# Cross attention: exponentials turned on VectorE in squares of 32 and moved between partitions by transfers, in place of transposes on TensorE

## The chip, the cores and the metric

One core of one Trainium2 chip. The metric is device time in microseconds (us) of the whole program, the median over several executions. Five engines work side by side: TensorE (PE in the profile, with PEld for its weight loads), VectorE (DVE), ScalarE (ACT), GpSimd (POOL) and SyncE (SP), whose queue issues all DMA transfers of this kernel. Each engine has its own queue of instructions and runs it in order; semaphores tie them together.

## The reference, cut to what matters

The program is a two-layer decoder in float32 on 8 batches of 128 tokens by 512 features: attention, an autocorrelation against a context and a mixture of low-rank experts in the first layer; attention, cross attention and a low-rank sum in the second, each with a residual and a layer norm. The change touches the cross attention of the second layer alone:

```python
B, Q, D = (8, 64, 512)
H, KV, HD = (16, 4, 96)
G = H // KV
b, q_len, _ = latents.shape                      # 8, 128
hidden = jnp.concatenate([context, latents], axis=1)   # 256 keys
q = (latents @ Wq.T).reshape(b, q_len, H, HD)
k = (hidden @ Wk.T).reshape(b, s_len, KV, HD)
v = (hidden @ Wv.T).reshape(b, s_len, KV, HD)
...
scores = jnp.einsum('bkgqd,bksd->bkgqs', q, k) * scale
attn = jax.nn.softmax(scores.astype(jnp.float32), axis=-1).astype(q.dtype)
out = jnp.einsum('bkgqs,bksd->bkgqd', attn, v)
out = out.reshape(b, H, q_len, HD).transpose(0, 2, 1, 3).reshape(b, q_len, H * HD)
return out @ Wo.T
```

Each of the 16 query heads has 128 queries against 256 keys; four query heads (G) share one of four key heads (KV).

## The kernel before

The kernel is written in a tile framework: tiles come from pools with a fixed number of buffers, and the framework derives all semaphores. It also orders each engine's instructions, by the order of the text and by when it reckons that operands are ready; so on ACT and DVE, and at places on PE, an instruction can stand before one that the text has earlier. The change leaves everything up to line 866 as it is.

**Cross attention.** Batches go in pairs (`pr`, `j`). A `Front` holds one pair's projections: transposed tokens xTx, context tokens cT (one DMA on SP, L749), values v, keys kT and queries qT. Its `pieces` (14 of them: tokens, four of values, three of keys, six of queries) are work that is cut up, so that `nxt.go(n)` puts n pieces of the next pair on PE between the steps of the present one.

**Heads8** is half a batch: two of the four query heads of each key head, so eight score maps (index j = 2g + u, with g the key head and u the head of the half). Its steps are:

- `__init__`: 48 matmuls s_x (L878) write the scores, 128 queries by 8 x 256 keys, into two PSUM tiles of two banks.
- `maxima` (L889, L890): two reductions of 1024 per lane on DVE.
- `exps(half)` for each of two halves: four exponentials on ACT (L900) with their row sums, a reciprocal on DVE (L904) and four multiplications in place (L906). The tile e is `[128, 8, 256]`: queries in partitions, then head, then key.
- `turn(pT)` brings the keys into partitions: for each g four transposes on PE (L915) into one PSUM bank, and an eviction of 128x512 into pT, by DVE for even g (L921) and by ACT for odd g (L923).

A batch has two Heads8 (hh = 0 and 1), the whole stage has 16. The tile pT has one buffer, e has two.

**mixed** (L932): with all of pT there, 48 matmuls o_x multiply the values with it, 32 output features of four key heads at a time, and three evictions write oT (L937). **projection** (pox, L86 within `mm_acc`) multiplies with the output weights, 24 matmuls, then `add_norm`. Together these two are `mix`, and a batch's `mix` runs in the next batch's first half, for the last batches later: the mix of batch 5 in batch 6's second half, that of batch 6 in batch 7's second half and that of batch 7 at the end.

**The loop** (L1015 to L1061) sets the order: in a batch's first half scores, the turn of the previous half (passed to `maxima`, which keeps the reductions behind it), exponentials, one piece, the previous batch's `mix`, one or two pieces; in its second half scores, first exponentials, three pieces, the turn of the first half, the other exponentials, two pieces. Batches 6 and 7 (`b >= B - 2`) have no next pair; there `low_rank()`, the small stage behind cross attention (xTf, pl, lT, pof), takes the place of the pieces.

**SP's queue** in this stage carries the cT load of each next pair (L749, when a `Front` is made) and the stores of finished batches (L992, L1082).

Of the kernel before, what the change touches and what calls it, by code (L numbers as in the profile page):

```python
# [17 lines left out]
P = 128  # L18
# [25 lines left out]
def decoder(ctx: ExitStack, tc: tile.TileContext, a: dict, out: bass.AP):  # L44
# [809 lines left out]
    with stage("x1b", 2, side="right") as ap, stage("f1", 2, side="right") as fp:  # L854
# [12 lines left out]
        class Heads8:  # L867

            def __init__(self, qT, kT, h0, name):
# [12 lines left out]
            def maxima(self, behind=None):  # L884

                self.m = sm.tile([P, 8], F32, tag="mx", name=f"m_{self.name}")
                with tc.issue_after(behind.ins) if behind else nullcontext():
                    for i in range(2):
                        nc.vector.tensor_reduce(self.m[:, 4 * i : 4 * i + 4], self.s[i], AX.X, ALU.max, negate=True)  # L889
                    nc.vector.tensor_scalar(self.m, self.m, 1.0 / math.sqrt(XD), None, ALU.mult)  # L890
                self.e = ap.tile([P, 8, 2 * P], F32, tag="e", name=f"e_{self.name}")
                self.su = sm.tile([P, 8], F32, tag="sux", name=f"su_{self.name}")
                self.rc = sm.tile([P, 8], F32, tag="rcx", name=f"rc_{self.name}")

            def exps(self, half):

                js = slice(4 * half, 4 * half + 4)
                for i in range(4):
                    j = 4 * half + i
                    nc.scalar.activation(  # L900
                        self.e[:, j, :], self.s[half][:, i, :], AF.Exp,
# [3 lines left out]
                for j in range(4 * half, 4 * half + 4):  # L905
                    nc.vector.tensor_scalar(self.e[:, j, :], self.e[:, j, :], self.rc[:, j : j + 1], None, ALU.mult)  # L906

            def turn(self, pT):

                for g in range(KV):  # L910
                    pt = bank(f"pt_{self.name}_{g}")
                    for s in range(2):
                        for u in range(2):
                            i = 2 * s + u
                            nc.tensor.transpose(  # L915
                                pt[:, i * P : (i + 1) * P], self.e[:, 2 * g + u, s * P : (s + 1) * P], ident
                            )
                    o = pT[:, :, g, self.h0 : self.h0 + 2, :].rearrange("p s u t -> p s (u t)")
                    i = pt.rearrange("p (s x) -> p s x", s=2)
                    if g % 2 == 0:  # L920
                        copied = nc.vector.tensor_copy(o, i)  # L921
                    else:
                        nc.scalar.copy(o, i)  # L923
                return copied

        def mixed(b, v, pT, oT):

            for n in range(NS):
                po = bank(f"o_x1_{b}_{n}")
                for s in range(2):  # L930
                    for g in range(KV):
# [3 lines left out]
                            rhs=pT[:, s, g].rearrange("p h t -> p (h t)"), start=(s == 0), stop=(s == 1),  # L935
                        )
                (nc.scalar.copy if n == 1 else nc.vector.tensor_copy)(oT[:, n, :], po)  # L937
# [57 lines left out]
        nxt = prev = None  # L995
# [19 lines left out]
        for b in range(B):  # L1015
# [4 lines left out]
            for hh in range(2):  # L1020
                now = Heads8(front.qT[:, :, toks], front.kT[:, :, :, toks], 2 * hh, f"x1_{b}_{hh}")
                if b >= B - 2:

                    now.maxima()
                    now.exps(0)
                    if hh == 0:
                        low_rank()
                        prev.turn(pT)
                        now.exps(1)
                        low_rank()  # L1030
                    else:
                        mix()
                        pT = ap.tile([P, 2, KV, G, P], F32, tag="pT", name=f"pT_x1_{b}", bufs=1)
                        prev.turn(pT)
                        now.exps(1)
                elif hh == 0:
                    now.maxima(prev.turn(pT) if prev else None)
                    now.exps(0)
                    now.exps(1)
                    if j == 0:  # L1040
                        nxt = Front(pr + 1)

                    nxt.go(1)
                    if mix:
                        mix()
                    nxt.go(1 + j)
                else:
                    now.maxima()
                    now.exps(0)
# [183 lines left out]
```

## Time and profile before

| | |
|---|---|
| median of 3 runs | 923.43 us (923.0 to 924.23) |
| the profiled execution | 920.14 us, of which its instructions span 918.3 us |
| granted TensorE clock, mean over the span | 0.996 |
| L915, transposes of e | 256, on PE 31.5 us busy together |
| L900, exponentials | 128 of 128x256, 488 ns each |
| L932, o_x | 384, 43.6 us busy together |
| L86, pox | 192, 84.5 us busy together |
| L749, cT load | 512 KB, lands 3.8 us after its issue |

Profile lines are read so: a line of kernel.py, the engine, the operation, the tile that it writes and those that it reads, shapes, how often; then busy time in us and the mean of one in ns; then the engine's idle time just before these instructions, and which engine and line ended it. In the chain of waits a piece is its start in us, its length in us, the engine, tile and line, and how many instructions. Times within the profile count from the first instruction of the profiled execution; its own time also holds what lies around the span.

Cross attention runs from 543 us to 901 us: s_x starts at 543.12, and the last pox ends at 901.2.

### The profile page before, as it was taken

To read this page: it belongs to the slowest core of one execution; us is meant where nothing else is said; L and a number is where in the kernel's file an instruction comes from. 1 tells how busy PE (TensorE), PEld (TensorE's weight loads), DVE (VectorE), ACT (ScalarE), POOL (GpSimd) and SP (SyncE) were. 2 spreads that over 40 slices of the span, in tenths; PEclk is the share of its full clock that TensorE was granted. 3 is DMA by queue.
4 is the path that set the end of the run, shared out by engine and by line. 5 is a ranking of instruction groups with operands and counts; after the bars stand their busy time and mean duration, and the time that the engine had idled before them with its cause. 6 is when DMAs were issued, how large, how long until landed. Compare 5 with 4: busy or idle time off the path is not lost.

```text
span 918.3 us, 17042 instructions
## 1 busy us (share of the span) xinstructions
PE 885.4 (96%) x6750; PEld 559.4 (61%) x6750; DVE 547.0 (60%) x1294; ACT 379.6 (41%) x1549; POOL 166.3 (18%) x235
## 2 busy tenths in 40 slices
PE   9999999899899999999999999999999999999985
PEld 5766656564445455565556787585758575865552
DVE  3757788886867668888887215433433353355544
ACT  3876564644232136666666022233223322334220
POOL 2401233233432423344330000000000000000001
PEclk9999999999999999999999999999999999999998
DMA  9700000121200020000030200000000000000000
GB/s 329 301 2 24 2 24 2 58 94 60 91 1 23 1 69 25 2 1 2 2 138 25 70 1 1 24 1 1 1 24 1 1 1 1 1 13 0 24 24 35
DMA packets 9298, 34.40 MB, mean 37 GB/s; under 512 B 1154, under 2 KB 1282, under 8 KB 7298
## 3 DMA queue, kind: packets, MB, share of 16 engines
q1 hardware_dynamic: 9218, 33.31, 10.0%
q8 instruction: 53, 0.87, 0.4%
q14 instruction: 27, 0.22, 0.1%
HBM read 31.21 MB, written 2.10 MB: 36 GB/s over the span
## 4 chain that ended last, share of the span: by engine, by line
PE 79%; DVE 10%; ACT 8%; issue 1%; POOL 1%; DMA 0%; POOLq 0%; SPq 0%; ACTq 0%; DVEq 0%
PE pox L86 9%; PE pqx L86 9%; PE pq L86 5%; PE s_x L878 5%; ACT e_a L193 5%; PE pk L86 5%; PE o_x L932 5%; PE pv L86 5%; PE pkx L86 5%; PE pvx L86 4%; PE pof L86 4%; PE pt_a L212 3%; PE pt_x L915 3%; PE s_a L164 2%; PE po L665 2%; PE o_a L229 1%
## 5 line engine op out<-in xcount | busy, mean ns | idle before, releaser
L193 ACT ACTIVATE e_a<-e_a,m_a 128x128 f32<-128x128 f32 (+1 forms) x512 | 184.8, 365 | 113.8 <-DVE m_a L181 113.8
L193 ACT ACTIVATION_READ_ACCUMULATOR e_a<-e_a,m_a 128x1 f32 x512 | 97.3, 190 | 0.0
L900 ACT ACTIVATE e_x<-s_x,m_x 128x256 f32<-128x256 f32 x128 | 59.1, 488 | 79.1 <-DVE m_x L890 79.1
L86 PE MATMUL pqx<-xTx,w_X_q 128*128 128x256 f32 x384 | 84.8, 380 | 0.0
L86 PE MATMUL pox<-w_X_o,oTx 128*128 128x512 f32 x192 | 84.5, 596 | 0.0
L86 PEld LDWEIGHTS pqx<-xTx,w_X_q 128*128 128x128 f32 x384 | 72.5, 190 | 11.9 <-issue 2.4
L889 DVE TENSOR_REDUCE m_x<-s_x 128x4 f32<-128x1024 f32 x32 | 37.6, 1217 | 54.1 <-PE s_x L878 54.1
L86 PEld LDWEIGHTS pox<-w_X_o,oTx 128*128 128x128 f32 x192 | 35.8, 190 | 48.8 <-issue 44.6
L97 POOL TENSOR_TENSOR rs_x<-ve_x,neghalf 128x1 f32<-128x1 f32 x8 | 4.4, 548 | 324.1 <-DVE ve_x L95 324.1
L181 DVE TENSOR_REDUCE m_a<-e_a 128x4 f32<-128x512 f32 (+1 forms) x128 | 62.6, 542 | 0.0
L792 ACT COPY qTx<-pqx 128x512 f32<-128x512 f32 x24 | 14.1, 588 | 105.8 <-PE pqx L86 105.8
L212 PE MATMUL pt_a<-ident,e_a 128*128 128x128 f32 x384 | 48.6, 274 | 4.9 <-DVE e_a L352 3.9
L878 PE MATMUL s_x<-kTx,qTx 32*128 32x256 f32 x768 | 50.3, 384 | 1.4 <-ACT e_x L900 1.4
L212 PEld LDWEIGHTS pt_a<-ident,e_a 128*128 128x128 f32 x384 | 43.5, 141 | 12.8 <-DVE e_a L352 4.9
L103 DVE TENSOR_TENSOR x_x<-pox,x_a 128x512 f32<-128x512 f32 x8 | 5.5, 692 | 70.5 <-PE pox L86 70.5
L923 ACT COPY pT_x<-pt_x 128x512 f32<-128x512 f32 x32 | 18.8, 591 | 67.8 <-PE pt_x L915 67.6
L878 PEld LDWEIGHTS s_x<-kTx,qTx 32*128 32x128 f32 x768 | 39.9, 184 | 11.2 <-issue 6.4
L932 PE MATMUL o_x<-pT_x,vx 128*32 128x512 f32 x384 | 43.6, 594 | 0.0
L921 DVE COPY pT_x<-pt_x 128x512 f32<-128x512 f32 x32 | 22.0, 687 | 32.0 <-PE pt_x L915 31.9
L164 PEld LDWEIGHTS s_a<-kbd,qT 32*64 32x64 f32 x1024 | 20.7, 131 | 28.1 <-issue 8.9
L906 DVE TENSOR_SCALAR e_x<-e_x,rc_x 128x256 f32<-128x256 f32 x128 | 36.5, 348 | 1.1
L164 PE MATMUL s_a<-kbd,qT 32*64 32x256 f32 (+1 forms) x1024 | 33.2, 335 | 1.8 <-DVE pT_a L213 0.8
(209 smaller groups left out, 1707.6 us busy)
## 6 DMA issues: line engine op xcount, KB each, us to landing
w_X_q<-in_X_q SPq DMA_DIRECT2D x3, 1024.0 KB, 5.1
w_X_o<-in_X_o SPq DMA_DIRECT2D x3, 1024.0 KB, 5.0
w_L_Wv<-in_L_Wv SPq DMA_DIRECT2D x2, 1024.0 KB, 6.3
w_L_Wo<-in_L_Wo SPq DMA_DIRECT2D x2, 1024.0 KB, 8.0
x_in<-in_x SPq DMA_DIRECT2D x8, 256.0 KB, 7.9
ct<-in_ctx SPq DMA_DIRECT2D x8, 256.0 KB, 4.4
cT<-in_ctxT SPq DMA_DIRECT2D x4, 512.0 KB, 3.8
out<-x_f SPq DMA_DIRECT2D x8, 256.0 KB, 2.0
```

Of the source, the lines that this page charges most:

```text
L86: nc.tensor.matmul(ps, lhsT=l, rhs=r, start=(i == 0), stop=(i == n - 1))
L164: nc.tensor.matmul(s[r // 2][64 * u : 64 * u + 64, r % 2, cols], lhsT=qT[rows, 64 - 64 * part : P - 64 * part], rhs=kbd[rows, :, :keys], s ...
L181: self.scored = nc.vector.tensor_reduce(self.m[:, part, rs, :], self.by_heads(part)[:, rs], AX.X, ALU.max, negate=True)
L193: nc.scalar.activation(e[:, r, x, :], e[:, r, x, :], AF.Exp, bias=self.m[:, part, r, x : x + 1], accum_out=self.su[:, part, r, x : x + 1],)
L212: nc.tensor.transpose(pt[:, r, cols], self.e[:, 2 * i + r, cols], ident)
L878: nc.tensor.matmul(sc[g // 2][:, g % 2, u * 256 : (u + 1) * 256], lhsT=qT[rows, (h0 + u) * NS + n, :], rhs=kT[rows, n], start=(n == 0), st ...
L889: nc.vector.tensor_reduce(self.m[:, 4 * i : 4 * i + 4], self.s[i], AX.X, ALU.max, negate=True)
L900: nc.scalar.activation(self.e[:, j, :], self.s[half][:, i, :], AF.Exp, bias=self.m[:, j : j + 1], scale=1.0 / math.sqrt(XD), accum_out=sel ...
L906: nc.vector.tensor_scalar(self.e[:, j, :], self.e[:, j, :], self.rc[:, j : j + 1], None, ALU.mult)
L915: nc.tensor.transpose(pt[:, i * P : (i + 1) * P], self.e[:, 2 * g + u, s * P : (s + 1) * P], ident)
L921: copied = nc.vector.tensor_copy(o, i)
L932: nc.tensor.matmul(po[32 * g : 32 * g + 32, :], lhsT=v[:, s, g * XD + 32 * n : g * XD + 32 * n + 32], rhs=pT[:, s, g].rearrange("p h t -> ...
```

## The change

The exponentials are laid out so that a key block of 32 is the outer index: e becomes `[128, 8, 8, 32]`, that is key block, head, key within the block. ACT and DVE write and read it in runs of 32 elements.

After the four multiplications of a half, one DVE transpose over `[128, 8, 4, 32]` turns every square of 32 queries by 32 keys in place: partition 32i + k then holds key 32a + k of block a, for the 32 queries of block i. What is left is to bring the square of key block a to the partitions 32 (a mod 4) and on. `turn` does that with 16 transfers on SP's queue, one for each pair (i, j) of query block and key block modulo 4: 32 partitions by two runs of 1 KB, 64 KB each, from e to pT. The tile pT becomes `[128, 2, 4, 2, 256]`: key half, query block, half of the heads, and head by query within the block.

`mixed` reads pT with runs of 64 columns, and its evictions put the columns back into the order that `projection` expects, in runs of 32.

The loop no longer carries a `prev`: a turn stands right after the second exponentials of its own half. In a batch's first half it stands behind the previous batch's `mix`, because pT has one buffer; in batches 6 and 7 both turns stand in the second half, behind `mix`. The reductions are no longer held behind a turn.

```diff
--- before.py
+++ after.py
@@ -868,6 +868,7 @@
 
 
 
+
             def __init__(self, qT, kT, h0, name):
                 self.h0, self.name = h0, name
                 sc = [banks(f"s_{name}_{i}") for i in range(2)]
@@ -881,14 +882,12 @@
                             )
                 self.s = [t.rearrange("p g (u k) -> p (g u) k", u=2) for t in sc]
 
-            def maxima(self, behind=None):
-
+            def maxima(self):
                 self.m = sm.tile([P, 8], F32, tag="mx", name=f"m_{self.name}")
-                with tc.issue_after(behind.ins) if behind else nullcontext():
-                    for i in range(2):
-                        nc.vector.tensor_reduce(self.m[:, 4 * i : 4 * i + 4], self.s[i], AX.X, ALU.max, negate=True)
-                    nc.vector.tensor_scalar(self.m, self.m, 1.0 / math.sqrt(XD), None, ALU.mult)
-                self.e = ap.tile([P, 8, 2 * P], F32, tag="e", name=f"e_{self.name}")
+                for i in range(2):
+                    nc.vector.tensor_reduce(self.m[:, 4 * i : 4 * i + 4], self.s[i], AX.X, ALU.max, negate=True)
+                nc.vector.tensor_scalar(self.m, self.m, 1.0 / math.sqrt(XD), None, ALU.mult)
+                self.e = ap.tile([P, 8, 8, 32], F32, tag="e", name=f"e_{self.name}")
                 self.su = sm.tile([P, 8], F32, tag="sux", name=f"su_{self.name}")
                 self.rc = sm.tile([P, 8], F32, tag="rcx", name=f"rc_{self.name}")
 
@@ -898,30 +897,22 @@
                 for i in range(4):
                     j = 4 * half + i
                     nc.scalar.activation(
-                        self.e[:, j, :], self.s[half][:, i, :], AF.Exp,
+                        self.e[:, :, j, :], self.s[half][:, i, :].rearrange("p (a k) -> p a k", k=32), AF.Exp,
                         bias=self.m[:, j : j + 1], scale=1.0 / math.sqrt(XD), accum_out=self.su[:, j : j + 1],
                     )
                 nc.vector.reciprocal(self.rc[:, js], self.su[:, js])
                 for j in range(4 * half, 4 * half + 4):
-                    nc.vector.tensor_scalar(self.e[:, j, :], self.e[:, j, :], self.rc[:, j : j + 1], None, ALU.mult)
+                    e = self.e[:, :, j, :]
+                    nc.vector.tensor_scalar(e, e, self.rc[:, j : j + 1], None, ALU.mult)
+                nc.vector.transpose(self.e[:, :, js, :], self.e[:, :, js, :])
 
             def turn(self, pT):
-
-                for g in range(KV):
-                    pt = bank(f"pt_{self.name}_{g}")
-                    for s in range(2):
-                        for u in range(2):
-                            i = 2 * s + u
-                            nc.tensor.transpose(
-                                pt[:, i * P : (i + 1) * P], self.e[:, 2 * g + u, s * P : (s + 1) * P], ident
-                            )
-                    o = pT[:, :, g, self.h0 : self.h0 + 2, :].rearrange("p s u t -> p s (u t)")
-                    i = pt.rearrange("p (s x) -> p s x", s=2)
-                    if g % 2 == 0:
-                        copied = nc.vector.tensor_copy(o, i)
-                    else:
-                        nc.scalar.copy(o, i)
-                return copied
+                e = self.e.rearrange("p (s j) h k -> p s j (h k)", s=2)
+                for i in range(4):
+                    for j in range(4):
+                        nc.sync.dma_start(
+                            pT[32 * j : 32 * j + 32, :, i, self.h0 // 2, :], e[32 * i : 32 * i + 32, :, j, :]
+                        )
 
         def mixed(b, v, pT, oT):
 
@@ -932,9 +923,13 @@
                         nc.tensor.matmul(
                             po[32 * g : 32 * g + 32, :],
                             lhsT=v[:, s, g * XD + 32 * n : g * XD + 32 * n + 32],
-                            rhs=pT[:, s, g].rearrange("p h t -> p (h t)"), start=(s == 0), stop=(s == 1),
+                            rhs=pT[:, s].rearrange("p i h x -> p (i h) x")[:, :, 64 * g : 64 * g + 64],
+                            start=(s == 0), stop=(s == 1),
                         )
-                (nc.scalar.copy if n == 1 else nc.vector.tensor_copy)(oT[:, n, :], po)
+                (nc.scalar.copy if n == 1 else nc.vector.tensor_copy)(
+                    oT[:, n, :].rearrange("p (h i t) -> p i h t", h=4, i=4),
+                    po.rearrange("p (i h t) -> p i h t", i=4, h=4),
+                )
 
         def projection(b, oT):
             po = bank(f"pox_{b}")
@@ -992,7 +987,7 @@
             nc.sync.dma_start(out[b], y)
 
         front.go(14)
-        nxt = prev = None
+        nxt = None
         done, tokens_low, scores_low = [], [], []
 
         def low_rank():
@@ -1019,40 +1014,36 @@
             toks = slice(j * P, (j + 1) * P)
             for hh in range(2):
                 now = Heads8(front.qT[:, :, toks], front.kT[:, :, :, toks], 2 * hh, f"x1_{b}_{hh}")
+                now.maxima()
+                now.exps(0)
                 if b >= B - 2:
 
-                    now.maxima()
-                    now.exps(0)
                     if hh == 0:
                         low_rank()
-                        prev.turn(pT)
                         now.exps(1)
                         low_rank()
+                        first = now
                     else:
                         mix()
-                        pT = ap.tile([P, 2, KV, G, P], F32, tag="pT", name=f"pT_x1_{b}", bufs=1)
-                        prev.turn(pT)
+                        pT = ap.tile([P, 2, 4, 2, 8 * 32], F32, tag="pT", name=f"pT_x1_{b}", bufs=1)
+                        first.turn(pT)
                         now.exps(1)
+                        now.turn(pT)
                 elif hh == 0:
-                    now.maxima(prev.turn(pT) if prev else None)
-                    now.exps(0)
-                    now.exps(1)
                     if j == 0:
                         nxt = Front(pr + 1)
-
+                    now.exps(1)
                     nxt.go(1)
                     if mix:
                         mix()
+                    pT = ap.tile([P, 2, 4, 2, 8 * 32], F32, tag="pT", name=f"pT_x1_{b}", bufs=1)
+                    now.turn(pT)
                     nxt.go(1 + j)
                 else:
-                    now.maxima()
-                    now.exps(0)
                     nxt.go(3)
-                    pT = ap.tile([P, 2, KV, G, P], F32, tag="pT", name=f"pT_x1_{b}", bufs=1)
-                    prev.turn(pT)
                     now.exps(1)
+                    now.turn(pT)
                     nxt.go(2)
-                prev = now
 
             def mix(b=b, v=front.v[:, j], pT=pT):
                 oT = ap.tile([P, NS, 512], F32, tag="oT", name=f"oTx_{b}", bufs=1)
@@ -1065,7 +1056,6 @@
 
         lT = turned_heads(B - 3, scores_low.pop()[1])
         ls = scored(*tokens_low.pop())
-        prev.turn(pT)
         mix()
         normed_last = add_norm.done
         lTs = [lT, turned_heads(B - 2, ls)]
```

## The prediction

> **What bounds the kernel now.** I read the page's engine sums first, then the stretches of the cross-attention stage, then its chain of waits in order of time.
>
> ```profile
> span 918.3 us, 17042 instructions
> PE 885.4 (96%) x6750; PEld 559.4 (61%) x6750; DVE 547.0 (60%) x1294; ACT 379.6 (41%) x1549; POOL 166.3 (18%) x235
> ```
>
> ```profile
> 543.00:808.00 265.00, 263.94 (x1701) 181.34 (x1704) 106.25 (x234) 74.61 (x244) 2.74 (x5) 1.00 0.02 5
> 808.00:918.00 110.00, 95.86 (x598) 54.68 (x590) 57.00 (x147) 30.85 (x109) 6.29 (x11) 0.97 0.06 20
> ```
>
> The columns are the stretch, its length, the busy time of PE, PEld, DVE, ACT and POOL, the granted clock, and DMA share and GB/s. From 543 to 808 TensorE never rests (263.9 of 265.0), DVE works 40% and the DMA engines 2%. After 808 PE has 14 us of holes, where batches 6 and 7 are left without other work. The chain over two halves of a batch:
>
> ```profile
> 694.83 2.80 PE s_x L878 x48
> 697.63 10.56 PE pqx L86 x48
> 708.19 1.75 PE pt_x L915 x16
> 709.94 3.46 PE pqx L86 x16
> 713.39 2.80 PE s_x L878 x48
> 716.20 1.90 PE pt_x L915 x16
> 718.09 0.87 PE pt_xTx L129 x8
> 718.97 5.29 PE o_x L932 x48
> 724.25 10.50 PE pox L86 x24
> ```
>
> Every piece is PE, end to end; pt_x is one turn(), 1.75 or 1.90 us. Whatever leaves PE here shortens the span, until something else is late.
>
> **What it removes.** All 256 transposes of L915 and their 64 evictions:
>
> ```profile
> L915 PE MATMUL pt_x<-ident,e_x 128*128 128x128 f32 x256 | 31.5, 275 | 0.0
> L921 DVE COPY pT_x<-pt_x 128x512 f32<-128x512 f32 x32 | 22.0, 687 | 32.0 <-PE pt_x L915 31.9
> L923 ACT COPY pT_x<-pt_x 128x512 f32<-128x512 f32 x32 | 18.8, 591 | 67.8 <-PE pt_x L915 67.6
> L906 DVE TENSOR_SCALAR e_x<-e_x,rc_x 128x256 f32<-128x256 f32 x128 | 36.5, 348 | 1.1
> L889 DVE TENSOR_REDUCE m_x<-s_x 128x4 f32<-128x1024 f32 x32 | 37.6, 1217 | 54.1 <-PE s_x L878 54.1
> ```
>
> On the chain stand eleven turns before 808 (six of 1.75, five of 1.90: 20.0 us) and after it 1.02, 1.75, 0.59 (there an eviction), 1.75 and 1.88: together 27.0 us. That is the gain; the 31.5 us of PE's own busy time is its upper end, since near 812 and 846 PE waits for ACT and DVE anyway. The evictions (22.0 us of DVE, 18.8 of ACT) are off the chain and count nothing.
>
> **What it adds on VectorE.** 32 transposes in place, 128x1024 each. The trace has none. The nearest row is the reduction that reads 1024 per lane, 1.22 us; the other end is a fixed instruction for each of its 32 squares, and the smallest DVE instruction (ve_x, 128x1) takes 0.154: 32 x 0.154 = 4.9. I take 1.24, because a transpose reads and writes each element once like the rows around it. The Trainium skill (VectorE: DVE Perf Modes, "The three transpose paths") gives 311 ns for 128x128 in bf16 on VectorE; eight of those would be an estimate of 2.5 us for 1024 columns, no run here shows it, and the sum by it would be about 913.
>
> Before 808 that is 22 x 1.24 = 27 us more on DVE against 15 us of copies less, in 159 us of idle time; what counts is only the delay of a half's exponentials. In the last stretch, where DVE and ACT set some of the steps, eight transposes (9.9 us) replace ten copies (6.9). I charge 1.0 of the 3.0 us difference (bounds 0 and 3).
>
> **What it adds on SP.** 16 transfers per turn, 64 KB each, 256 in all, on a queue that in this stage carries two loads and eight stores.
>
> ```profile
> 1.16 0.89 SPq L287 DMA_DIRECT2D xT<-in_xT  x2
> 2.10 0.43 SPq L299 DMA_DIRECT2D vecs<-in_vecs  x1
> 2.57 0.43 SPq L282 DMA_DIRECT2D w_L_Wk<-in_L_Wk  x1
> 3.04 0.43 SPq L301 DMA_DIRECT2D masks<-in_masks  x1
> 12.25 8.73 SPq L314 DMA_DIRECT2D x_in<-in_x  x8
> out<-x_f SPq DMA_DIRECT2D x8, 256.0 KB, 2.0
> ```
>
> Unhindered issues follow each other by 0.47 us whatever their size (vecs is 4 KB). The eight x_in loads came 1.09 apart: each waits for the transfer eight places before it (L314 waits for w_L_Wv, the ninth issue, as the seventeenth), and the load was full. A quiet 256 KB transfer lands 2.0 us after its issue, well inside eight issues (3.8 us), so I take 0.47 and 2.0: a turn takes 15 x 0.47 + 2.0 = 9.1 us from its release. The other end is 1.09: 15 x 1.09 + 2.0 = 18.4. Against it the Trainium skill (DMA: Bandwidth & Descriptors, "Bandwidth") asks for 1 MiB per transfer and lists 0.95 us for 64 KB; if that were the pace, the sum would be an estimated 932; the trace's issues at 0.47 speak against such a pace, though none is within SBUF.
>
> Is the turn late? It needs both halves of the exponentials. Where the next batch is even (b = 1, 3): scores start at 694.83, the first half is normalized at 703.64, the second at 705.95; with two transposes between, 12.6 us after the start. Landed: 12.6 + 9.1 = 21.7. PE without the transposes is at the next mix after 2.80 + 10.56 + 3.46 + 2.80 + 0.87 = 20.5. Late by 1.2, twice: 2.4 us. Where the next batch is odd (b = 0, 2, 4; starting at 737.33): second half normalized at 747.96, so 13.1 with the transposes, landed at 22.2; PE arrives after 2.80 + 7.94 + 6.91 + 2.80 + 3.46 = 23.9. Hidden, by 1.7. Batch 5's mix comes a half later (822.50, 35 us after its scores). Batch 7's e is normalized at 863.9; its 16 transfers queue behind the 16 of the first half, which wait for o_x of batch 6 to free pT (860.5): 860.5 + 7.5 + 7.5 + 2.0 = 877.5, and mix 7 would start at 884.6 less the two turns before it, 881.0. Hidden, by 3.5.
>
> **Added waits.** The pT tile is single, so SP stands in front of each first half's turn until the mix before has read it; behind it in the queue are only the other half's turn and the next pair's cT load, which lands in 3.8 us and is read after a mix of 15.8. The first matmul of a mix now waits for transfers on eight semaphores; an additional wait on PE's queue is an EVENT_SEMAPHORE of 51 ns (L164), so 7 x 51 = 0.36 us, eight times 2.9; PE's queue runs ahead of its matmuls, so between 0 and 2.9: I take 1.6.
>
> **Costed at nothing.** o_x now reads runs of 64 columns at a stride of 1 KB; the 128-column form of L164 reads two runs of 64 that lie 2 KB apart, in 274 ns, like the 273 of a contiguous transpose. If each o_x grew by a tenth: 43.6 us / 10 = 4.4. Strided writes on DVE: L646 writes runs of 16 in 680 ns against 687 for a plain copy. For ACT's exponentials in runs of 32 there is no row; if each of a half's eight took L906's pace longer (four in 1.14 us, 0.285 each), the turns would be 2.3 later: 2 x 2.3 + 3 x 0.6 = 6.4 us.
>
> **Sum.** 27.0 - 1.0 - 2.4 - 1.6 = 22.0 us. The profiled execution took 920.14 around its span of 918.3, the median of the runs is 923.43; the same difference on the median: **901.4**.
>
> **Rivals.**
> 1. *Fully covered.* The order on the engines is not that of the text: in the trace exponentials overtake query copies, and matmuls of a next half start between low-rank pieces. If values(0,0) (2.58 us) is put before the mix and the semaphores are hidden: 27.0 - 1.0 = 26.0, **897**.
> 2. *Transposes at half speed*, 2.5 us: turns 2.5 later, 2 x 3.7 + 3 x 0.8 = 9.8; in the last stretch some 5; with 1.6 for the semaphores 27.0 - 16.4 = 10.6, **913**. For it: nothing of this kind is in the trace. At 4.9 us it would end above 923.
> 3. *The transfers set the pace* (slower). Lateness is 2 x (1.2 + x) + 3 x (x - 1.7) for turns later by x, and it eats the 24.4 that are left at x = 5.4, that is from 0.83 us a transfer on. At the 1.09 of x_in: x = 9.3, 21.0 + 22.8 = 43.8, so 19.4 slower, **943**. For it: each waits for the eighth before. Against: x_in moved four times the bytes, from HBM, behind some 5 MB of other loads.
> 4. *Queue order.* If transposes stand before the evictions of v, k and oT that PE's four banks wait for, 1.24 us a turn: 16 x 1.24 = 20 at worst, half of it likely, 22.0 - 10 = 12, **911**. Against: in the steady stretch DVE idles 60%.
>
> **How the numbers follow.** Forecast 0.38, its own range 896 to 908 (below: neither lateness nor semaphores nor charge in the last stretch; above: the 6.4 of slower exponentials); rival 1 0.13; rival 2 0.19; rival 3 0.20; rival 4 0.10. About 0.2% (1.8 us) is what a measurement can tell from nothing. Slower: 0.17 of rival 3, 0.04 each of 2 and 4: 0.25; same 0.03; faster 0.72. The range runs from 893 (all of the 31.5 less 1.0) to 930, which leaves out 0.03 below and 0.16 above, most of rival 3.
>
> **What would show it.** Right: no L915; DVE transposes near 1.24; SP issues 0.47 apart and landing about 2 us after; o_x waiting for a transfer only in batches 2 and 4, about a microsecond; PE's busy time down by some 31. Wrong: o_x idle for several microseconds with a DMA named as releaser in every batch (rival 3), a transpose row above 2 us (rival 2), PE idle behind DVE copies (rival 4), or an o_x group that costs more than 43.6.

## The result, and the profile after

| | before | after |
|---|---|---|
| median, shared runs on one chip | 923.01 us (921.14 to 924.24, 10 runs) | 928.11 us (925.09 to 929.3, 10 runs) |
| the profiled execution, span | 920.14, 918.3 us | 925.09, 923.2 us |
| granted TensorE clock, mean | 0.996 | 0.980 |
| from the first scores of batch 0 to those of batch 6 | 543.12 to 806.07: 262.9 us | 544.40 to 808.10: 263.7 us |
| from there to the end of the span | 112.2 us | 115.1 us |

The ratio of after to before is 1.0052, 95% interval 1.0038 to 1.0067: slower by half a per cent, where 901.4 us was forecast. The two last rows divide the span where the next pair's projections end. The forecast's terms, divided in the same way (the 1.6 for semaphores as 0.2 for each of eight mixes, five of them before batch 6), give 246.3 (262.9 - 20.0 for eleven turns + 2.4 of lateness + 1.0) and 106.8 (112.2 less 7.0 for five turns, plus 1.0 for VectorE and 0.6). So 17.4 us are missing before batch 6 and 8.3 after it; another 1.3 us were lost before the stage began.

Engine sums and the clock row of the page of after:

```profile
span 923.2 us, 16947 instructions
PE 870.3 (94%) x6494; PEld 538.1 (58%) x6494; DVE 564.0 (61%) x1294; ACT 361.7 (39%) x1517; POOL 166.3 (18%) x235
PEclk9999999999999999999999999998999999989898
```

TensorE has 256 instructions less, but its busy time fell by 15 us, not by the 31.5 that they took: some of what is left became dearer. The clock row, full up to the end before, now has dips from the 28th slice on. The groups that answer to the removed ones, and the new issue row (64 KB each, 2.0 us from issue to landing):

```profile
L923 PE MATMUL o_x<-pT_x,vx 128*32 128x512 f32 x384 | 47.9, 651 | 17.5 <-DMA pT_x<-e_x 17.5
...
L907 DVE STREAM_TRANSPOSE e_x<-e_x 128x1024 f32<-128x1024 f32 x32 | 39.8, 1242 | 0.8
...
pT_x<-e_x SPq DMA_DIRECT2D x256, 64.0 KB, 2.0
```

The new DVE transpose takes the 1.24 us that were assumed and a transfer lands after the 2.0 that were assumed. But o_x sat idle for 17.5 us before it, with a transfer named as releaser, where 2.4 had been charged; and its own busy time rose from 43.6 to 47.9 us. The chain of waits through the mix of batch 1 (start, length, what) shows why:

```profile
603.51 2.81 PE s_x L879 x48
...
608.99 1.94 ACT e_x L899 x8
...
611.35 1.15 DVE e_x L906 x4
612.53 1.25 DVE e_x L907
...
613.87 1.15 DVE e_x L906 x4
615.05 1.26 DVE e_x L907
616.32 0.58 SPq L913
...
616.95 0.60 SPq L913
...
617.59 0.59 SPq L913
...
618.23 1.56 SPq L913
...
619.83 0.60 SPq L913
...
626.86 2.01 DMA pT_x<-e_x
...
629.01 7.60 PE o_x L923 x48
```

From the scores to the release of the turn is 12.8 us, as worked out (12.6). Then SP is the bound: an issue takes 0.595 us (the median of all 256), and the next starts 0.64 after it, with one of 1.56 among them; sixteen of them and the landing take 12.5 us here, and 11.6 to 12.9 in the other turns, not 9.1. PE arrives at 624.1, waits until 629.01, and then o_x takes 7.60 us instead of 5.36. The stretches of a trace (start to end, length, busy time and instructions of PE, PEld, DVE, ACT and POOL, the granted clock, DMA share and GB/s) tell the reason of the last:

```profile
543.00:808.00 265.00, 247.96 (x1495) 163.47 (x1493) 119.04 (x236) 61.41 (x221) 2.74 (x5) 0.98 0.22 49
808.00:923.00 115.00, 96.89 (x547) 51.86 (x546) 61.11 (x145) 26.21 (x100) 6.43 (x11) 0.90 0.25 62
...
626.80:633.50 6.70, 4.49 (x24) 1.35 (x28) 0.78 (x2) 2.75 (x13) 0.00 (x0) 0.50 0.14 29
722.40:725.70 3.30, 2.57 (x14) 0.71 (x18) 0.00 (x0) 2.22 (x10) 0.00 (x0) 0.50 0.06 13
818.00:824.70 6.70, 6.56 (x19) 4.32 (x19) 3.26 (x9) 1.21 (x5) 0.00 (x0) 0.50 0.01 2
852.10:858.80 6.70, 6.68 (x25) 4.85 (x23) 5.07 (x14) 1.29 (x7) 0.04 (x1) 0.50 0.35 92
889.60:892.90 3.30, 3.01 (x16) 0.91 (x20) 0.27 (x1) 0.00 (x0) 0.00 (x0) 0.50 0.35 127
```

In five stretches of the stage the granted clock is exactly half. The first, second and last begin within waits of o_x (of 4.86, 3.86 and 1.52 us). The third and fourth lie in batches 6 and 7, and there PE is busy 6.56 and 6.68 of 6.70 us: it isn't waiting then, it works at half speed. Before, these stretches ran at full clock, and what stood there were, among others, the transposes of `turn`. So there are two suspects: SP's pace, and a clock that falls when PE has too little to do. The Trainium skill ("TensorE: Matmul & The Clock Gate", Part 1) describes the second: TensorE's clock halves after an idle window of some 3.4 us of a free-running monitor. The half-clock stretches here last 3.41 or 6.83 us each, and they begin 28, 56, 66 and 77 times 3.413 us behind the first of the five, which agrees. "Idle" must not be taken as fully at rest, though: in the 3.41 us before each of the five PE was busy for 0.80, 0.35, 1.56, 1.59 and 1.77 us. Nor is PE's busy time alone the rule: two slices of the same raster from 575.56 on held 1.66 and 1.63 us, and the clock stayed whole behind them.

### The profile page after: what moved, and what is told of

It reads as the page before. It is cut to its first block, busy times and chain, and to the rows that moved or that the text cites. A ratio compares the mean times of both kernels' runs of the same rounds, so it can differ in the third digit from the quotient of the medians.

```text
span 923.2 us, 16947 instructions
## 1 busy us (share of the span) xinstructions
PE 870.3 (94%) x6494; PEld 538.1 (58%) x6494; DVE 564.0 (61%) x1294; ACT 361.7 (39%) x1517; POOL 166.3 (18%) x235
## 4 chain that ended last, share of the span: by engine, by line
PE 63%; DVE 15%; ACT 10%; SPq 7%; issue 2%; DMA 2%; POOL 1%; POOLq 0%; DVEq 0%; ACTq 0%
PE pox L86 8%; SPq L913 7%; PE pqx L86 6%; ACT e_a L193 6%; PE o_x L923 5%; PE pq L86 5%; PE pk L86 4%; PE pv L86 4%; PE pof L86 4%; PE s_x L879 3%; PE pt_a L212 3%; PE pvx L86 2%; PE po L665 2%; PE s_a L164 2%; DVE e_x L907 2%
## 5 line engine op out<-in xcount | busy, mean ns | idle before, releaser
L899 ACT ACTIVATE e_x<-s_x,m_x 128x256 f32<-128x256 f32 x128 | 58.9, 485 | 116.8 <-DVE m_x L889 63.9
L923 PE MATMUL o_x<-pT_x,vx 128*32 128x512 f32 x384 | 47.9, 651 | 17.5 <-DMA pT_x<-e_x 17.5
L879 PE MATMUL s_x<-kTx,qTx 32*128 32x256 f32 x768 | 53.5, 388 | 5.1 <-ACT e_x L899 5.1
L879 PEld LDWEIGHTS s_x<-kTx,qTx 32*128 32x128 f32 x768 | 41.8, 186 | 18.0 <-ACT e_x L899 8.3
L212 PEld LDWEIGHTS pt_a<-ident,e_a 128*128 128x128 f32 x384 | 43.5, 141 | 12.8 <-DVE e_a L352 4.9
L923 PEld LDWEIGHTS o_x<-pT_x,vx 128*32 128x32 f32 x384 | 13.9, 119 | 46.8 <-issue 33.3
L907 DVE STREAM_TRANSPOSE e_x<-e_x 128x1024 f32<-128x1024 f32 x32 | 39.8, 1242 | 0.8
L164 PEld LDWEIGHTS s_a<-kbd,qT 32*64 32x64 f32 x1024 | 20.7, 131 | 28.1 <-issue 8.9
```

What stands on the lines that cost most here:

```text
L164: nc.tensor.matmul(s[r // 2][64 * u : 64 * u + 64, r % 2, cols], lhsT=qT[rows, 64 - 64 * part : P - 64 * part], rhs=kbd[rows, :, :keys], s ...
L212: nc.tensor.transpose(pt[:, r, cols], self.e[:, 2 * i + r, cols], ident)
L879: nc.tensor.matmul(sc[g // 2][:, g % 2, u * 256 : (u + 1) * 256], lhsT=qT[rows, (h0 + u) * NS + n, :], rhs=kT[rows, n], start=(n == 0), st ...
L899: nc.scalar.activation(self.e[:, :, j, :], self.s[half][:, i, :].rearrange("p (a k) -> p a k", k=32), AF.Exp, bias=self.m[:, j : j + 1], s ...
L907: nc.vector.transpose(self.e[:, :, js, :], self.e[:, :, js, :])
L923: nc.tensor.matmul(po[32 * g : 32 * g + 32, :], lhsT=v[:, s, g * XD + 32 * n : g * XD + 32 * n + 32], rhs=pT[:, s].rearrange("p i h x -> p ...
```

## The experiments

The same two stretches for every run, from its trace, with the median and the ratio to the kernel before, measured beside it (the median of before was 923.09, 922.10, 922.87 and 924.28 us for e1 to e4, e5 to e8, e9 to e11 and e12):

| run | median us | ratio, 95% interval | batch 0 to 6 | rest | o_x waits for transfers |
|---|---|---|---|---|---|
| after | 928.11 | 1.0052 [1.0038, 1.0067] | 263.7 | 115.1 | 17.5 |
| e1 no transfers | 907.17 | 0.9811 [0.9784, 0.9837] | 243.9 | 115.3 | none |
| e2 two queues | 907.43 | 0.9829 [0.9808, 0.9850] | 246.2 | 112.1 | 2.2 |
| e3 one run | 925.56 | 1.0031 [1.0015, 1.0046] | 264.0 | 114.9 | 14.3 |
| e4 mix later | 911.31 | 0.9873 [0.9858, 0.9888] | 249.3 | 115.5 | 5.1 |
| e5 e2 and e4 | 905.48 | 0.9813 [0.9790, 0.9837] | 243.9 | 114.7 | none |
| e6 e2, ten added matmuls | 907.86 | 0.9848 [0.9830, 0.9866] | 246.8 | 114.4 | 2.8 |
| e7 e5, ten added matmuls | 905.25 | 0.9820 [0.9805, 0.9836] | 243.9 | 114.4 | none |
| e8 all partitions | 906.83 | 0.9833 [0.9813, 0.9853] | 246.2 | 114.7 | 0.9 |
| e9 e5, five added matmuls | 897.93 | 0.9732 [0.9713, 0.9750] | 243.9 | 108.0 | none |
| e10 after, five added matmuls | 923.71 | 1.0006 [0.9994, 1.0018] | 265.5 | 112.5 | 15.1 |
| e11 e5, transposes thrice | 932.53 | 1.0099 [1.0086, 1.0112] | 258.2 | 126.6 | 5.2 |
| e12 e5, other order | 902.20 | 0.9773 [0.9758, 0.9788] | 243.9 | 112.4 | none |

**e1: are the transfers the cause at all?** `turn` issues nothing, and pT is filled once.

```diff
-                for i in range(4):
-                    for j in range(4):
-                        nc.sync.dma_start(
-                            pT[32 * j : 32 * j + 32, :, i, self.h0 // 2, :], e[32 * i : 32 * i + 32, :, j, :]
-                        )
+                return
...
+        pT = ap.tile([P, 2, 4, 2, 8 * 32], F32, tag="pT", name="pT_once", bufs=1)
+        nc.gpsimd.memset(pT, 1.0 / 256)
```

> All 256 transfers are left out; the matmuls o_x read a tile of constants that is written once before the stage, so the cross attention's mix has the wrong weights in it, while exponentials, multiplications and transposes on VectorE stay. Theory: o_x waits 17.5 us for transfers, and the waits (PE idle 2 to 5 us) cost more by the half granted clock that follows three of them, some 5 us; without transfers both go, 928 - 22 = about 906, and the half clock stays only near 818 and 852, where the low-rank stage leaves PE little work. Rival, the VectorE transposes cost the gain (delayed exponentials or evictions): the time stays above 920.

907.17. The transfers cost the changed kernel 21 us, and in the traces the gain lies before batch 6 (263.7 to 243.9); the rest stays at 115. So the transfers explain the first missing 17.4 us. Of the second 8.3 they can explain at most the last mix (1.5 us of waiting and 1.5 of half clock in o_x); e1 has neither and takes as long, with half clock for 10.2 us in batch 7 where the changed kernel has 6.8.

**e2: issue, or transfer?** If SP's issuing sets the pace, a second issuing queue halves the turn; if the transfers themselves did, it would change nothing.

```diff
-                        nc.sync.dma_start(
+                        (nc.scalar if j % 2 else nc.sync).dma_start(
```

> Half of the 16 transfers of a turn (odd key blocks) are issued from ScalarE's queue, the others stay on SyncE's. Theory, the pace of issue on one queue (0.64 us a transfer) makes a turn 12.5 us long: eight places at 0.64 and 2.0 for landing are 7.1 us, turns land before PE comes, the 17.5 us of waits fall below 3, about 908. Rival, the transfers themselves (landing, engines, semaphores) set the pace: issues on the two queues slow each other to 1.2 us, turns stay above 11 us, 925 to 930.

907.43, about as good as with no transfers. The page of e2:

```profile
L923 PE MATMUL o_x<-pT_x,vx 128*32 128x512 f32 x384 | 42.9, 594 | 2.2 <-DMA pT_x<-e_x 2.2
...
pT_x<-e_x ACTq DMA_DIRECT2D x128, 64.0 KB, 2.3
pT_x<-e_x SPq DMA_DIRECT2D x128, 64.0 KB, 2.2
```

A transfer lands hardly later with two under way (2.2 and 2.3 us against 2.0), a turn takes 7.0 to 8.5 us instead of 11.6 to 12.9, and o_x is back at 42.9 us busy: with the waits gone, its clock is whole too. The Trainium skill ("DMA: Bandwidth & Descriptors", "Rules for kernel authors") says that spreading transfers over issuing engines doesn't help bandwidth and only saves the sequencer's issue time. The second half holds here, and was worth 20.7 us; of the first no run here can tell, since none was short of bandwidth (a DMA share of 0.24 before batch 6 in e2).

**e3: is it the shape of the transfer?** One run of 2 KB per partition in place of two of 1 KB (key blocks in the order j, s in e and pT).

```diff
-                self.e = ap.tile([P, 8, 8, 32], F32, tag="e", name=f"e_{self.name}")
+                self.e = ap.tile([P, 4, 2, 8, 32], F32, tag="e", name=f"e_{self.name}")
...
-                            pT[32 * j : 32 * j + 32, :, i, self.h0 // 2, :], e[32 * i : 32 * i + 32, :, j, :]
+                            pT[32 * j : 32 * j + 32, i, self.h0 // 2, :], e[32 * i : 32 * i + 32, j, :]
```

> The key half becomes the inner index of e and of pT, so that each transfer moves one run of 2 KB per partition instead of two runs of 1 KB; same bytes, same count. Theory, the second dimension makes an issue 0.60 long against 0.33 to 0.43 for the loads of one run per partition: the pace falls to 0.40 to 0.47, a turn to 8 to 9 us, the waits of 17.5 us to about 3 to 5, some 3 us of half clock go with them, 911. Rival, 0.64 belongs to the 32 partitions or to transfers within SBUF: pace and time stay, 926 to 930.

A miss: 925.56. In its trace an issue still takes 0.59 us at the median and the turns 11.4 to 12.9. Half the runs make no cheaper issue.

**e4: the same lateness, met from the other side.** The previous batch's mix goes behind one more group of pieces, so PE comes to it later.

```diff
                     nxt.go(1)
+                    nxt.go(1 + j)
                     if mix:
                         mix()
...
                     now.turn(pT)
-                    nxt.go(1 + j)
```

> In a batch's first half the previous batch's mix stands behind the one or two pieces that follow it in the changed kernel (values, 2.6 us, or two query pieces, 6.9 us); nothing else moves. Theory: the waits of batches 0, 2, 4 (3.5, 2.1, 1.7 us) vanish, those of batches 1 and 3 (4.9, 3.9) fall by 2.6 each, the half clock after these goes, 928 - 12.5 - 3.5 = about 912. Rival, PE's waits are only the sign of a stage bound by VectorE, ScalarE and SyncE: the wait moves to another instruction, above 922.

911.31, as the theory: the turns are as long as in the changed kernel (11.6 to 12.8 us), but o_x waits 5.1 us instead of 17.5:

```profile
PE o_x L923 <- DMA pT_x<-e_x: 5.1, 3, 2.1
```

**e5: both.** The edits of e2 and e4 together.

> The transfers alternate between SP and ACT, and the mix stands behind one more group of the next pair's projections. Theory (with two queues o_x waits for transfers only 2.2 us in all, so the lateness is gone; what is left above the forecast is the clock in the last stretch, which neither edit touches): 904 to 908, within 3 us of the 907.4 of two queues alone, and o_x waits for no transfer. Rival (the two gains of 20.7 and 16.8 us come from different places and add): below 898.

905.48, the theory's. From batch 0 to batch 6 it takes 243.9 us, to a tenth what e1 takes without any transfer: 19.1 less than before, of the 20.0 us of transposes that stood there. That part is finished. What is left is the rest, 114.7 us against 106.8 forecast, and e1 has the same. No transfer is to blame for it.

**e6 and e7: the clock.** Matmuls whose result nobody reads are put where PE waits for the first exponentials of batches 6 and 7; e6 is e2 with ten of them, e7 is e5 with ten.

```diff
                     if hh == 0:
                         low_rank()
+                        po = bank(f"hold_{b}")
+                        for _ in range(10):
+                            nc.tensor.matmul(po[:8, :], lhsT=now.m, rhs=wb, start=True, stop=True)
                         now.exps(1)
```

> Two queues, and in batches 6 and 7 ten added matmuls (m times the low-rank weights, 8 partitions out, a result that nobody reads) while PE waits for the exponentials of the first half. Theory (the half clock after 801 and 835 in the run with two queues comes from PE's rest there, and it costs some 3 us after the first and 2 after the second): no granted clock of 0.5 between 800 and 845, pl back from 1.66 to 0.89 us for six, 901 to 904. Rival (the half clock follows something else, or the steps of that stretch are set by ACT and DVE whatever PE's clock): 906 or more.

> All three: two queues, the mix one group later, the ten added matmuls in batches 6 and 7. Theory: 900 to 904, about the forecast of 901.4, since both missing terms (issue pace and clock) are then gone. Rival (the mix's later place leaves PE short of work elsewhere): above 906.

The half clock was gone, as the theory said (none from 243 us to the last 9 us of the span, mean 0.995 and 0.993), and six pl took 0.96 us again. But the time stayed: 907.86, as e6's rival had it, and 905.25, between the two cases of e7. The ten took 8.75 us, 0.875 each, and PE reached pt_lT 12.1 us after the end of the first scores of batch 6, instead of 8.3 in e2. What the clock gave, the filler took.

**e8: whose is the issue time?** The same bytes and number of transfers, from all partitions to the same partitions.

```diff
-                e = self.e.rearrange("p (s j) h k -> p s j (h k)", s=2)
-                for i in range(4):
-                    for j in range(4):
-                        nc.sync.dma_start(
-                            pT[32 * j : 32 * j + 32, :, i, self.h0 // 2, :], e[32 * i : 32 * i + 32, :, j, :]
-                        )
+                e = self.e.rearrange("p j h k -> p (j h k)").rearrange("p (n x) -> p n x", x=P)
+                for n in range(16):
+                    nc.sync.dma_start(pT[:, n // 8, n // 2 % 4, self.h0 // 2, n % 2 * P : n % 2 * P + P], e[:, n])
```

> The same 16 transfers a turn of 64 KB each on SP, but each from all 128 partitions to the same 128 partitions, 512 bytes in each; the squares thus do not change rows, which is the part left out. Theory (an issue's 0.595 us belongs to a transfer of 32 partitions; the loads with 128 partitions took 0.33 to 0.43): busy 0.33 to 0.43, pace at most 0.47, a turn 8 to 9 us, o_x waits less than 5 us in all, 905 to 910. Rival (every transfer within SBUF costs SP 0.6 to issue, whatever its form): pace 0.64 and 923 to 929 as the changed kernel.

Neither case as stated. The pace is the rival's: 0.60 an issue, turns of 11.4 to 12.9 us. The time is the theory's, 906.83, for a reason that neither had. The chain of e8, where the turn of the same half as above begins:

```profile
610.05 0.42 SPq L912
610.52 0.60 SPq L912
611.16 0.60 SPq L912
...
614.38 1.93 SPq L912
```

It starts 10.4 us after its scores (599.64), not 12.8: a transfer here carries the heads of one `exps` half and goes when that half is turned. And each writes only one half s of the keys, so the first matmuls of o_x (s = 0) go after eight of them: o_x of this batch began at 620.28, while the last transfer landed at 622.80. That is read from the trace; it was not tried for itself.

**e9: five in place of ten.** The same as e7 with `range(5)`.

> Two queues, the mix one group later, and five added matmuls in batches 6 and 7 in place of ten (ten took 8.75 us, 0.875 each, and PE went on with pt_lT 3 to 4 us later than without them). Theory (ten kept the clock but outlasted the wait; five, 4.4 us, end before the wait does): no granted clock of 0.5 from 790 to 880 and pt_lT after the first scores of batch 6 within 8.5 us (12.1 with ten), 899 to 903. Rival (that stretch is set by ACT and DVE, so that neither the clock nor the added work counts): 904.5 to 906.5 as with ten and with none.

897.93, 0.9732 of before: a little below the forecast, and the fastest of all runs. PE of e9 behind the first scores of batch 6 (start, length):

```profile
793.50 0.60 PE L129 MATMUL pt_xTf<-ident,x_x 128*128 128x128 f32 x4
794.03 4.46 PE L1025 MATMUL hold<-wf,m_x 128*8 128x512 f32 x10
798.50 0.30 PE L974 MATMUL pt_lT<-ident,ls 128*128 128x128 f32 x1
...
799.27 0.96 PE L955 MATMUL pl<-wf,xTf 128*128 128x136 f32 x6
```

(Each matmul in float32 is two instructions in the profile, so the five stand as ten.) The five end just as ls is there, and pt_lT comes 7.9 us after the end of the scores. But the added matmuls had also moved something: the framework's order now has the next half's scores behind the low-rank pieces, but for 4 of the 48 in batch 7; in e5, 14 of the 48 stood ahead of them in batch 6 and 16 in batch 7.

**e12: that order without the matmuls.** It takes the confound out of e9.

```diff
+                with tc.issue_after(low_sum.done.ins) if hh and b >= B - 2 else ExitStack():
                     now = Heads8(front.qT[:, :, toks], front.kT[:, :, :, toks], 2 * hh, f"x1_{b}_{hh}")
...
-            nc.tensor.matmul(po, lhsT=lT, rhs=wb, start=True, stop=True)
+            low_sum.done = nc.tensor.matmul(po, lhsT=lT, rhs=wb, start=True, stop=True)
```

> Two queues and the mix one group later, without added matmuls; the second half's scores of batches 6 and 7 are put behind the low-rank pieces (after pof), the order on PE that the five added matmuls had brought with them. Theory (the 7.5 us between 905.5 and 897.9 are the clock): half clock again at about 800 and 835, 904 to 908. Rival (they are the order of the scores, not the clock): 896 to 900 with or without half clock.

902.20, between the two cases. The same place in e12, with two lines of DVE:

```profile
793.57 0.60 PE L129 MATMUL pt_xTf<-ident,x_x 128*128 128x128 f32 x4
798.56 0.45 PE L974 MATMUL pt_lT<-ident,ls 128*128 128x128 f32 x1 [4.39 <-DVE rc_x L903]
...
799.91 1.73 PE L955 MATMUL pl<-wf,xTf 128*128 128x136 f32 x6
```

```profile
796.94 1.25 DVE L907 STREAM_TRANSPOSE e_x<-e_x 128x1024 f32<-128x1024 f32 x1
798.11 0.31 DVE L967 SCALAR_TENSOR_TENSOR ls<-pl,rc,lg 128x128 f32<-128x128 f32 x1
```

and the stretches 790 to 825 of e9 and of e12:

```profile
790.00:825.00 35.00, 34.32 (x245) 18.01 (x238) 23.15 (x50) 11.20 (x43) 1.10 (x2) 1.00 0.33 74
```

```profile
790.00:825.00 35.00, 29.94 (x217) 17.01 (x211) 21.31 (x47) 11.13 (x42) 0.96 (x2) 0.90 0.33 75
```

pt_lT stands at the same place in both, 10.7 us after the scores began. (The profile names rc_x as what ended its wait; ls, which pt_lT reads, was done at 798.42, just before.) In e12 PE has waited 4.39 us for it and then runs at half clock: six pl take 1.73 us instead of 0.96, and the next scores start 16.0 us after the first, in e9 13.6. By the ratios, e12 is 0.9813 - 0.9773 = 0.0040, or 3.7 us, below e5, and e9 another 0.9773 - 0.9732 = 0.0041, or 3.8 us, below e12, each within 2 to 3 us by the intervals. The traces say what of this is clock and what is order (us):

| run | batch 6, first scores to o_x | batch 7, the same | from there to the end | half clock in batch 6 and 7 |
|---|---|---|---|---|
| before | 16.4 | 15.2 | 63.1 | none |
| after | 19.5 | 18.8 | 61.0 | 6.8 and 6.8 |
| e2 | 19.6 | 19.0 | 57.7 | 6.8 and 6.8 |
| e5 | 19.3 | 20.3 | 59.3 | 6.8 and 10.2 |
| e12 | 18.8 | 18.9 | 58.9 | 6.8 and 6.8 |
| e9 | 16.4 | 17.0 | 58.8 | none |

From e12 to e9 the two batches lose 2.4 and 1.8 us and elsewhere they differ by 0.2 at most: that is the clock, and in batch 6 the order is the same in both. From e5 to e12 it is less clear. Of 3.6 us in the spans, 1.3 lie before the stage, where the code is the same, and in batch 7 e5 has half clock for 3.4 us longer. Against e2, which has e5's order after batch 6 and as much half clock as e12 in the two batches, the new order shows 0.8 and 0.2 us. So the order is worth about 1 us where it can be seen alone; the rest of the 3.7 is not shown to be its doing.

**e10: the five in the changed kernel.** One queue, the mix at its place. The edit is that of e9's added matmuls alone, and it brings the same change of order.

> The changed kernel with the five added matmuls alone: one queue, the mix at its place. Theory (clock in the last stretch worth 3 to 5 us; the waits for transfers and the half clock behind them stay): 922 to 925.5, half clock at about 627, 722 and 890 but not at 818 and 852. Rival: 927 to 929.

923.71, as the theory: by the ratios 0.0046 less than the changed kernel, 4.2 us. After batch 6 the trace has 2.6 us less (112.5 against 115.1), and the clock was whole in 815 to 822 and 850 to 858. Before it, the waits for transfers (15.1 us) and the half clock behind them are still there; that stretch took 1.8 us more, with half clock for 6.83 us instead of 3.41 at 721. (The profiled execution of after lies 3 us below its median, that of e10 at its median, so the spans differ by less than the medians.)

**e11: are the DVE transposes off the path?** Each done three times, in e5.

```diff
-                nc.vector.transpose(self.e[:, :, js, :], self.e[:, :, js, :])
+                for _ in range(3):
+                    nc.vector.transpose(self.e[:, :, js, :], self.e[:, :, js, :])
```

> Two queues, the mix one group later, and every VectorE transpose done three times (the third gives what the first gave), 2.5 us more a half group, 80 us more of DVE in all. Theory (with the turns at 7 to 8.4 us the mixes of batches 1 and 3 have 2 us to spare and the others more, so that before 808 some 2 x 3 us come on the path and in the last stretch up to 8): 911 to 920 against 905.5 without. Rival (the transposes are on the path in each of the 16 halves): 905.5 + 32 x 2.5 = 985, or half of it, above 940.

932.53, between the two cases: 27 us for 79 us of DVE, 14.3 of them before batch 6. So at three times the load the transposes are partly on the path; what a single one costs the run does not tell. The chain of e11 shows what neither case had reckoned:

```profile
574.37 1.22 DVE e_x L908
...
576.98 0.76 DVE e_x L906 x3
577.74 0.60 DVE kTx L784
578.34 1.15 DVE e_x L908
579.50 0.58 DVE kTx L784
580.07 1.16 DVE e_x L908
```

The transposes share DVE's queue with the evictions of kT (L784) and of oT, and PE then waits: 3.7 us in all for oT alone. It is rival 4's mechanism, at three times the load. Part of the 27 us is clock again: between the stage's start and the last 10 us of the span e11 has half clock for 41 us, e5 for 20.

## Why the prediction was wrong, point by point

**The step that failed** is the pace of SP: "Unhindered issues follow each other by 0.47 us whatever their size". The rows under it were loads from HBM, the only ones that the trace had. Transfers within SBUF are issued in 0.595 us and 0.64 apart (0.59 to 0.60 and 0.63 to 0.64 in all three shapes tried), with one of over 1 us in seven of the sixteen turns. A turn takes 11.6 to 12.9 us in place of 9.1. The term of 2.4 us was mis-sized for it: with x = 3.4 us, that of batch 1's turn of 12.5, the forecast's own formula gives 2 x (1.2 + 3.4) + 3 x (3.4 - 1.7) = 14.3, and the waits before batch 6 measured 16.0 (3.53, 4.86, 2.08, 3.86 and 1.66). Rival 3 had the mechanism, and reckoned that lateness alone eats the gain from 0.83 us a transfer on. At the measured pace, 24.4 - 14.3 = 10.1 us should have been left.

**The step that was missing** took most of those: nothing was charged for the clock. The forecast treated PE's removed work as pure gain. The waits that replaced it brought half clock behind them (o_x at 7.60, 6.63 and 6.87 us in place of 5.36 is 5.0 us), and in batches 6 and 7, where no transfer was late until the last mix, half clock came once the transposes were gone. e10 puts that at 4.2 us with the order that came with it; e9 against e12 at some 4 us for the clock alone. A place that was called "holes" in the reading of before, 14 us of PE's rest after 808, was the sign: the clock held there until 911 us before, and no longer after the change.

**How it adds up.** Before batch 6, 13.6 us of longer waits (16.0 less 2.4), 3.5 of half clock in o_x (7.60 and 6.63 in place of 5.36) and 0.9 of removal that no run shows (19.1 in e5, of 20.0), less the 1.0 for semaphores, make 17.0 of the 17.4 that are missing. After it, batches 6 and 7 took 19.5 and 18.8 us from their scores to o_x, where the removal of 1.02 and 0.59 from 16.4 and 15.2 leaves 15.3 and 14.6; so each is 4.2 us longer, not shorter. That is 8.4 us, and the tail another 1.5, less the 1.6 charged there: 8.3.

**The order in the last stretch** was charged nowhere either. About 1 us of it is shown (e12 against e2); the 3.7 us between e5 and e12 have differences of the clock in them. Without the turns, the framework placed the next half's scores ahead of the low-rank pieces, where they wait for the exponentials' PSUM, and the pieces wait behind them.

**Right were** the removal (19.1 us of the 20.0 before batch 6, once the turns are in time), the time of the transpose (1.242 us, against 1.24 taken), the landing (2.0), the release of the turn (12.8 after the scores, against 12.6), and nothing for the strided operands (o_x 42.9 in e2 against 43.6). Too high was the term for eight semaphores: where transfers were in time, as in e5, no wait of its own shows, and e5 takes as long before batch 6 as e1 without transfers (243.9). VectorE does 24 transposes before batch 6, not the 22 that were counted; nothing rested on it. The charge of 1.0 us for DVE in the last stretch can't be told apart in these runs. The estimate of 2.5 us from the Trainium skill's 311 ns for 128x128 in bf16 ("VectorE: DVE Perf Modes", "The three transpose paths") is refuted by the 1.242 us, for 1024 columns in float32. What a transpose does to others is visible in e12, where ls of the low-rank part follows a transpose of 1.25 us on DVE (796.94), and pt_lT waits for ls.

**Of the misses among the expectations**, e3 and e8 held that an issue's time comes from its shape; both say no. What it does come from is open: a transfer within SBUF took 0.59 to 0.60 us at the median and every load or store in the stage 0.33 to 0.53, on SP; no run varied source and destination alone. Open is also why the removal before batch 6 gives 19.1 us and not 20.0, and the half clock of 3.41 us before the stage that every kernel but the profiled execution of before shows somewhere between 113 and 243; it sits at different places in kernels whose code is the same up to there, and the stage starts 0.9 to 3.5 us later in these kernels than in before; how much of that is the clock was not tried.

## What to carry to other kernels

Price a queue's issues by a row of the same kind of transfer, and where none exists, take the range seriously: sixteen small issues in series on one queue are a latency of their own, which a second queue (e2) or a later reader (e4) took away here. When work leaves the bounding engine, look at the places where that engine was barely busy enough: on TensorE the clock can halve there, as it did here, and make what remains dearer. A few matmuls that nobody reads can hold the clock, if they end before the wait does; in this kernel ten that outlasted it gave nothing, five gave 4 us.

## What the runs showed of the hardware

- The issue of a transfer within SBUF held SP for 0.59 to 0.60 us at the median in three forms of 64 KB (32 partitions with two runs of 1 KB, 32 with one of 2 KB, 128 with one of 512 bytes), and ACT for 0.61; loads and stores of HBM in the stage took 0.33 to 0.53, and the first unhindered ones of the program 0.43.
- In seven of the sixteen turns of the changed kernel one issue took 1.1 to 1.6 us (up to 1.9 in e8), and transfers around it landed after 3 to 4 us instead of 2. In the trace a packet of 16 KB on the instruction queue, of 0.9 to 1.5 us, lies at the same moment in all seven (618.20 beside the issue at 618.23). That is a coincidence in time, and not tested.
- A clock that halved stayed so for 3.41 us or two to four times that (3.41, 6.83, 10.24, in e11 13.65), and began on a raster of 3.41 us that lies differently in each execution; e2 and e5, with the same code after batch 6, differ there by 2.6 us, with half clock for 13.7 and 20.5 us before the last 10 us of the span.
- No full rest is needed for it: in e5 it halved at 870.22 behind 3.41 us in which PE was busy for 1.98 and never waited longer than 1.43.
